# Four layers on one core: layer 3's sums in the scores' PSUM banks, another setup of layer 0, weights loaded within layer 0, and z's bias written into its bank by ScalarE

## The chip, the cores and the metric

The kernel runs on one core of one Trainium2 chip. The metric is the device time of one execution in microseconds, the median of several runs; lower is better. The profile of one execution has a span some 10 us under the median.

## The reference

64 graphs with 256 nodes and 256 features pass through four layers, each followed by a residual addition and a layer norm: `x = norm(x + layer(x, adj))`. All is float32.

- Layer 0 is a recurrence over the 256 nodes, for all graphs at once. Step i computes

```
x_par = sum_j adj[j, i] / d_j * h_j        # d_j: row sums of adj
r, z  = sigmoid(x_i @ W_ioux.T + b + x_par @ W_iouh.T + b)
hc    = tanh(x_i @ W_coux.T + b + (x_par * r) @ W_couh.T + b)
h_i   = z * x_par + (1 - z) * hc
```

  where `h_j` is the new state for j < i and the input for j >= i.
- Layer 1 is a graph convolution: `relu(D^-1/2 adj D^-1/2 (x W1.T + b1))`.
- Layer 2 is attention with one head and `adj` as a soft mask, followed by `Wo`, a bias and a relu.
- Layer 3 is attention with 8 heads of 32 features, with a score kept where `adj > 0`, then `Wo` and a bias.

## The kernel before

**Layer 0** (`_recurrence`). A setup loads and turns the weights, splits the bias into three bf16 parts (`bias3`) and writes the masks `window`. Then the part that doesn't depend on the recurrence, the contribution of the inputs to the first 128 nodes, is computed for all graphs in groups of GB = 8: `A` (L193) and `Xs` (L194) are loaded, `A` is masked on GpSimd, two matmuls a graph give `pb`, copies (half DVE, half ScalarE, L208) bring it to `ub`, and `x_out` stores it to DRAM `Us`. Then `degrees(0)` loads the first 32 rows of `adj` in four pieces through one buffer and computes `dinv`. `sums_in` loads from `Us` the accumulators `ACC` for 8 nodes each.

A step n, written out by hand (from here on each engine works in the order of the program): `xp` is transposed (`flip`), `h_part` adds its products with the weights to the PSUM tiles `rc` (gates r and c) and `z`, ScalarE takes the sigmoids, `rx` is transposed and gives c's second part, ScalarE takes tanh, DVE forms `zcc` (L815) and the next `xp` (L818). Between these PE computes the input products of the next step (`x_part`, L582). `rc` gets its bias by a ScalarE copy of `bias_rc` (L789), `z` by two small matmuls (`bias_part`, L573). Pushes of a new state into the accumulators of later nodes run on DVE (`ACC` L615) and GpSimd (`far` L647, `ACC` L651). States go through the tiles `hs` to a ring `Hw` of 64 nodes in SBUF (`into_ring`, in the steps p = n % 8 > 3) and from there to DRAM `Hd` (`flush`). Older states reach later nodes as "late" and "early" products, whose results pass through DRAM; `next_of(copies)` copies them out of PSUM on ScalarE, and `next_load` issues queued loads, two a step where p < 4.

**Layers 1 to 3** (`_layers`). All weights are loaded after the recurrence, W1 is turned, and the value bias of layer 3 is multiplied into its output bias (`bv`, L896 to L900). Then rounds: each advances five graphs, L, A, B, C and E, by one stage each, in the order of the string `ROUND`; `A.xT.1` is `Graph.xT(1)` of the graph in stage A. PSUM has four banks with the tag "mm", taken in turn by all products and transpositions (`bank`, `flipped`, `product` L948), and four, "sc0" to "sc3", for layer 3's scores (`s3`), one for each of four heads. `o3` takes two "mm" banks, and fills them with the sums of the exponentials (L1155) and the weighted values (L1164); `d3` divides on DVE (L1178 to L1180), `f3` applies `Wo`. `degrees_a` and `degrees_b` compute layer 1's `dis` (L1014), which `adT` needs on ScalarE.

A last part, `_layer_3`, runs only where a sum overflowed; it isn't entered here.

Of the kernel before, what the change touches and what calls it, by code (L numbers as in the profile page):

```python
# [19 lines left out]
P = 128  # L20
# [50 lines left out]
def _recurrence(tc, ident, Hd, x, adj, W_ioux, b_ioux, W_iouh, b_iouh, W_coux, b_coux, W_couh, b_couh):  # L71
# [31 lines left out]
    with ExitStack() as ctx:  # L103
# [6 lines left out]
        bias_rc = const.tile([P, 2, P], F32, name="bias_rc")  # L110
        tri = const.tile([P, P], F32, name="tri")
# [12 lines left out]
        with tc.tile_pool(name="r_setup", bufs=1) as tmp, tc.tile_pool(  # L124
            name="r_setup_ps", bufs=2, space=bass.MemoryType.PSUM
        ) as tps:
            for WT, wi, wc, s in ((WxT, W_ioux, W_coux, "x"), (WhT, W_iouh, W_couh, "h")):
                _load_wT(nc, tmp, tps, wi, ident, lambda c: WT[:, :, c % 2, c // 2 * 2, :], "i" + s)
                _load_wT(nc, tmp, tps, wc, ident, lambda c: WT[:, :, c, 1, :], "c" + s)
            bx, bh = (tmp.tile([1, 2, 3, P], F32, name=f"bias_{s}") for s in "xh")  # L130
            for t, bi, bc in ((bx, b_ioux, b_coux), (bh, b_iouh, b_couh)):
                for g in range(2):
                    nc.scalar.dma_start(
                        t[:, :, 2 * g, :],
                        bi[g * D:(g + 1) * D].rearrange("(c d) -> c d", c=2).unsqueeze(0),
                    )
                nc.scalar.dma_start(t[:, :, 1, :], bc.rearrange("(c d) -> c d", c=2).unsqueeze(0))
            nc.vector.tensor_add(bx, bx, bh)
            _split_bf16(nc, tmp, bias3, bx, "bias")

            span = tmp.tile([W, T // U, U], F32, name="span")
            nc.gpsimd.memset(span, 1.0)
            nc.gpsimd.affine_select(
                out=span, in_=span, pattern=[[U, T // U], [0, U]], compare_op=ALU.is_ge,
                fill=0.0, base=W - T // 2 - LAG - 1, channel_multiplier=-1,
            )
            for w in range(2):
                first = (w * T - W + T // 2) % W  # L150
                for lo, hi, at in ring(first, first + W):
                    for g in range(2):
                        nc.sync.dma_start(
                            window[w][g * W + at:g * W + at + hi - lo],
                            span[lo - first:hi - first].rearrange("p a u -> p (a u)"),
                        )
# [26 lines left out]


        with tc.tile_pool(name="r_first", bufs=2) as tmp, tc.tile_pool(
            name="r_first_ps", bufs=4, space=bass.MemoryType.PSUM
        ) as tps:
            for g in range(0, B, GB):
                A = tmp.tile([P, 2, GB, P], F32, tag="A", name=f"xA_{g}")
                Xs = tmp.tile([P, 2, GB, D], F32, tag="X", name=f"xX_{g}")  # L190
                for jc in range(2):
                    rows = slice(jc * P, (jc + 1) * P)
                    nc.sync.dma_start(A[:, jc], adj[g:g + GB, rows, 0:P].rearrange("b j i -> j b i"))  # L193
                    nc.scalar.dma_start(Xs[:, jc], x[g:g + GB, rows, :].rearrange("b j d -> j b d"))  # L194
                nc.gpsimd.tensor_mul(
                    A[:, 0], A[:, 0], tri.unsqueeze(1).to_broadcast([P, GB, P])
                )
                for n in range(0, GB, 4):
                    ub = tmp.tile([P, 4, D], F32, tag="ub", name=f"xu_{g}_{n}")
                    for e in range(0, 4, 2):  # L200
                        pb = tps.tile([P, 2, D], F32, tag="x", name=f"xp_{g}_{n}_{e}")
                        for q in range(2):
                            b = n + e + q
                            x_product(
                                pb, q, [A[:, jc, b, :] for jc in range(2)],
                                [Xs[:, jc, b, :] for jc in range(2)],
                            )
                        (nc.vector.tensor_copy if e else nc.scalar.copy)(ub[:, e:e + 2, :], pb)  # L208
                    x_out(0, g + n, ub)

        blk = ctx.enter_context(tc.tile_pool(name="r_blk", bufs=2))
        stream = ctx.enter_context(tc.tile_pool(name="r_stream", bufs=2))
        work = ctx.enter_context(tc.tile_pool(name="r_work", bufs=2))
        ps = ctx.enter_context(tc.tile_pool(name="r_ps", bufs=1, space=bass.MemoryType.PSUM))
# [24 lines left out]
        def load_later(out, in_, rank):  # L239

            begun = []

            def f(n):
                nc.sync.dma_start(out, in_)
                begun.append(n)

            loads.append((rank, f))
            loads.sort(key=lambda e: e[0])
            return begun
# [17 lines left out]
        def degrees(k):  # L267
# [16 lines left out]
            nc.vector.tensor_scalar(zero, deg, 0.0, None, ALU.is_equal)  # L284
            nc.vector.tensor_add(deg, deg, zero)
            nc.vector.reciprocal(deg, deg)
            nc.vector.tensor_scalar(zero, zero, -1.0, 1.0, ALU.mult, ALU.add)
            nc.vector.tensor_mul(deg, deg, zero)
            yield
            for h in range(2):  # L290
                at = k * T + h * HT
                for c in range(2):
                    nc.sync.dma_start(dinv[c * B:(c + 1) * B, at:at + HT], deg[h * B:(h + 1) * B])
# [69 lines left out]
        def early_load(e, got=[]):  # L363
# [5 lines left out]
            Hs = stream.tile([P, GB, D], F32, tag="Hs", name=f"Hs_{k}_{lo}_{t}", bufs=4)  # L369
# [258 lines left out]
        def state(n):  # L628
# [3 lines left out]
            hs = new("hs", n, 7)  # L632
# [4 lines left out]
        def into_ring():  # L637
            n, hs = ring_in.pop(0)
            for o in range(2):
                nc.sync.dma_start(Hw[n % W::W, :, o * P:(o + 1) * P], hs[o * B:(o + 1) * B])  # L640
# [19 lines left out]
        for _ in degrees(0):  # L660
            pass
        tables[0]["S"], double = load_S(0)
        double()
        tables[0]["Sd"] = chain_S(0)
        tables[0]["An"] = late_load(0)
        for a in range(3):
            sums_in(a)

        xq = {0: load_x(0)}
# [3 lines left out]
        xq[1] = load_x(1)  # L673
        rc = ps.tile([P, 2, P], F32, tag="rc", name="rc_0", bufs=2)
        z = ps.tile([P, P], F32, tag="z", name="z_ps_0")
        for G, gates in ((rc, slice(0, 2)), (z, 2)):
            bias_part(G, gates)
            if G is rc:
                nc.scalar.copy(bias_rc, rc)
# [29 lines left out]
        for now in range(N):  # L709
# [9 lines left out]
            if n:  # L719
# [13 lines left out]
                if p > 3:  # L733
# [67 lines left out]
            if not last:  # L801
# [6 lines left out]
                bias_part(z, 2)  # L808
# [29 lines left out]
            if i == 24:  # L838
                flush(n - 8 - T, n - 8)
            early_ahead(n)  # L840
# [14 lines left out]
        flush(N - T // 2, N)  # L855


def _layers(tc, ident, Hd, Yd, x, adj, w1, b1, l2, l3, out):
# [8 lines left out]
    nc = tc.nc  # L867
    B, N, D = x.shape
# [5 lines left out]
    with ExitStack() as ctx:  # L874
        const = ctx.enter_context(tc.tile_pool(name="l_const", bufs=1))
        W1T = const.tile([P, 2, D], F32, name="W1T")
        W2 = {n: _load_w(nc, const, l2["W" + n], f"W2{n}") for n in "qkvo"}
        W3 = {n: _load_w(nc, const, l3["W" + n], f"W3{n}") for n in "qkvo"}
        b1_r = _load_row(nc, const, b1, "b1_r")
        b2_r = _load_row(nc, const, l2["bo"], "b2o_r")  # L880
        b3_r = _load_row(nc, const, l3["bo"], "b3o_r")
        cols = const.tile([P, 6, 2], F32, name="b_cols")
        for s, b in enumerate((l2["bq"], l2["bk"], l3["bq"], l3["bk"], l3["bv"], l2["bv"])):
            _load_col(nc, cols[:, s, :], b)
# [5 lines left out]
        with tc.tile_pool(name="l_setup", bufs=1) as tmp, tc.tile_pool(  # L890
            name="l_setup_ps", bufs=2, space=bass.MemoryType.PSUM
        ) as tps:
            _load_wT(nc, tmp, tps, w1, ident, lambda c: W1T[:, :, c * P:(c + 1) * P], "w1")

            bv = tmp.tile([P, 2, P], F32, name="bv3")
            nc.vector.tensor_copy(bv, cols[:, 4, :].unsqueeze(2).to_broadcast([P, 2, P]))  # L896
            pb = tps.tile([P, D], F32, tag="wt", name="bv3_ps")
            for k in range(2):
                nc.tensor.matmul(pb, bv[:, k, :], W3["o"][:, k, :], start=(k == 0), stop=(k == 1))
            nc.vector.tensor_add(b3_r, b3_r, pb)  # L900
# [5 lines left out]
        ctx.enter_context(tc.manual_schedule())  # L906
# [23 lines left out]
        def bank(name, shape=(P, 2, D)):  # L930
            return ps.tile(list(shape), F32, tag="mm", name=name, bufs=4)

# [40 lines left out]
        class Graph:  # L973
# [7 lines left out]
            def load(self):  # L981
                b = self.b
                self.y = io.tile([P, 2, D], F32, tag="y", name=f"y_{b}", bufs=7)
                nc.sync.dma_start(self.y, Hd[:, b, :].rearrange("(c p) d -> p c d", p=P))
# [3 lines left out]
                nc.sync.dma_start(self.ad, adj[b].rearrange("(c p) m -> p c m", p=P))  # L988

# [158 lines left out]
            def o3(self):  # L1148


                self.o_ps = [bank(f"o3_{self.b}_{hc}") for hc in range(2)]
# [241 lines left out]
```

## Time and profile before

| | |
|---|---|
| time, median of 3 | 3578.55 us (3575.83 to 3585.26) |
| span of the profile | 3568.9 us |
| mean granted TensorE clock | 0.977 |
| busy: PE, DVE, ACT, POOL | 3223.1, 2465.2, 1900.3, 1874.5 us |
| chain that ended last | PE 61%, DVE 14%, DMA 6%, issue 6%, POOL 6%, ACT 5% |
| HBM read and written | 224.01 and 99.61 MB |

The busy times are over the whole span, whose stages have different limits. Four stages can be told apart in the slices of the page: the setup up to some 156 us, the steps of the recurrence up to 1563 us, a passage with little work up to some 1676 us, and the rounds up to the end. In the profile PE is a matmul, PEld a weight load, DVE VectorE, ACT ScalarE, POOL GpSimd, SPq the queue that issues DMAs from SyncE. An arrow names what a row reads or waits for.

### The profile page before, as it was taken

Reading aid. Unit: us, or ns where it says so; the run is one execution under the profiler, and the core shown is the slowest. Engines: PE = TensorE matmul, PEld = TensorE weight load, DVE = VectorE, ACT = ScalarE, POOL = GpSimd, SP = SyncE. Lnnn points to the kernel's source line nnn. Section 1 sums busy time; section 2 is a strip of 40 time slices with the busy share of each in tenths; the row PEclk is TensorE's granted clock in tenths of the full one; section 3 lists DMA queues with packets and bytes.
Section 4 is the critical chain, followed back from the end, with each engine's and each line's share of the span. In section 5 each row is a group of like instructions: output and inputs, shape, how many; then the busy total and the mean of one; then the engine's idle time right before and its main releaser. Section 6 shows DMA issues by size and latency. Waiting matters only on the chain.

```text
span 3568.9 us, 80419 instructions
## 1 busy us (share of the span) xinstructions
PE 3223.1 (90%) x29350; PEld 2318.4 (65%) x29350; DVE 2465.2 (69%) x7052; ACT 1900.3 (53%) x5026; POOL 1874.5 (53%) x2181
## 2 busy tenths in 40 slices
PE   5599999999989898858999999999999999999998
PEld 4455555555555555536777777777777777777775
DVE  2366767767667777735777777777777777777776
ACT  0155545545445454424666666666666666666664
POOL 2266677767667778723444444444444444444443
PEclk9799999999999999978999999999999999999999
DMA  8846566787876564140111111111111111111100
GB/s 281 224 132 144 162 174 152 162 190 201 201 191 166 154 152 120 58 116 18 45 45 45 45 45 45 45 45 45 45 45 45 45 45 45 45 43 45 45 27 22
DMA packets 389637, 348.43 MB, mean 98 GB/s; under 512 B 107244, under 2 KB 355192, under 8 KB 384120
## 3 DMA queue, kind: packets, MB, share of 16 engines
q1 hardware_dynamic: 367280, 323.84, 34.0%
q10 hardware_dynamic: 21960, 19.41, 1.6%
q8 instruction: 235, 3.85, 0.4%
q14 instruction: 162, 1.33, 0.1%
HBM read 224.01 MB, written 99.61 MB: 91 GB/s over the span
## 4 chain that ended last, share of the span: by engine, by line
PE 61%; DVE 14%; DMA 6%; issue 6%; POOL 6%; ACT 5%; SPq 2%; ACTq 0%; DVEq 0%; POOLq 0%
PE mm L948 13%; PE rc L590 4%; DVE p L1141 4%; PE s L1132 4%; PE rc L582 3%; PE mm_g L948 3%; PE mm_t L948 3%; PE mm_3f L948 3%; PE mm_3v L948 3%; PE mm_2s L948 3%; PE mm_2v L948 3%; PE late L506 3%; DVE ACC L615 3%; PE mm_2w L948 3%; POOL ACC L651 2%
## 5 line engine op out<-in xcount | busy, mean ns | idle before, releaser
L615 DVE SCALAR_TENSOR_TENSOR ACC<-keep,S,ACC 128x128 f32<-128x128 f32 x1712 | 504.8, 345 | 187.4 <-ACT hs L633 170.0
L1144 POOL TENSOR_TENSOR p3s<-p 128x256 f32<-128x256 f32 x512 | 387.8, 788 | 329.6 <-ACT p L1142 329.3
L925 ACT ACTIVATE y<-y,shift,rstd 128x256 f32<-128x256 f32 x512 | 273.4, 593 | 303.9 <-DVE shift L923 259.9
L1044 POOL TENSOR_TENSOR y<-y,g 128x512 f32<-128x512 f32 x64 | 81.1, 1267 | 601.1 <-issue 590.2
L651 POOL TENSOR_TENSOR ACC<-ACC,far 128x384 f32<-128x384 f32 (+1 forms) x313 | 371.3, 1186 | 24.6
L582 PE MATMUL rc<-WxT,xqT 128*64 128x256 f32 x2048 | 326.3, 397 | 6.1 <-ACT lb L232 1.7
L1141 DVE TENSOR_TENSOR p<-s,neg 128x512 f32<-128x512 f32 x512 | 317.7, 683 | 10.9 <-PE s L1132 8.8
L755 POOL TENSOR_TENSOR ready<-ACC,dinv 128x128 f32<-128x128 f32 x255 | 101.9, 400 | 391.3 <-DVE ACC L615 372.4
L647 POOL TENSOR_TENSOR far<-hs,S 128x384 f32<-128x384 f32 (+1 forms) x313 | 304.3, 972 | 4.7
L1142 ACT ACTIVATE p<-p 128x512 f32<-128x512 f32 x512 | 294.6, 624 | 2.6 <-DVE p L1141 1.6
L913 DVE BATCH_NORM_STATS2 st<-y 128x6 f32<-128x256 f32 x512 | 209.0, 408 | 95.0 <-POOL y L1044 90.2
L917 POOL TENSOR_TENSOR rstd<-rstd,mhalf 128x2 f32<-128x2 f32 x256 | 173.6, 695 | 125.7 <-DVE rstd L916 122.2
L1178 DVE RECIPROCAL rT<-o 128x256 f32<-128x256 f32 x128 | 223.8, 1748 | 0.3 <-PE o L1155 0.2
L599 ACT COPY xpT<-xpT_ps 128x128 f32<-128x128 f32 x256 | 68.3, 267 | 254.9 <-PE xpT_ps L597 254.9
L1164 PE MATMUL o<-p,v 128*32 128x256 f32 x2048 | 138.4, 382 | 70.8 <-ACT xT L1030 70.8
L590 PE MATMUL rc<-WhT,xpT 128*64 128x128 f32 x2048 | 170.7, 288 | 28.8 <-ACT xpT L599 28.6
L590 PEld LDWEIGHTS rc<-WhT,xpT 128*64 128x64 f32 x2048 | 108.1, 137 | 118.6 <-ACT xpT L599 84.1
L1187 DVE TENSOR_TENSOR y<-y,mm_3f 128x512 f32<-128x512 f32 x64 | 44.0, 688 | 187.9 <-PE mm_3f L948 187.9
L582 PE MATMUL z_ps<-WxT,xqT 128*64 128x128 f32 x2048 | 170.0, 287 | 0.0
L1107 ACT ACTIVATE qk<-mm,b_cols 128x256 f32<-128x256 f32 x256 | 107.5, 471 | 115.9 <-PE mm L948 115.9
L506 PE MATMUL late<-Hw,An 64*32 64x256 f32 x3840 | 154.9, 389 | 9.3 <-issue 4.4
L815 DVE TENSOR_TENSOR zcc<-zc,rc 128x128 f32<-128x128 f32 x256 | 72.7, 284 | 130.0 <-ACT rc L813 129.3
(168 smaller groups left out, 8004.6 us busy)
## 6 DMA issues: line engine op xcount, KB each, us to landing
xX<-in_x_dram ACTq DMA_DIRECT2D x16, 1024.0 KB
Us<-xu SPq DMA_DIRECT2D x64, 256.0 KB
rows<-in_adj_dram SPq DMA_DIRECT2D x64, 256.0 KB
ACC<-Us SPq DMA_DIRECT2D x32, 512.0 KB
xq<-in_x_dram SPq DMA_DIRECT2D x64, 256.0 KB
Hw<-hs SPq DMA_DIRECT2D x512, 32.0 KB
Es<-eu SPq DMA_DIRECT2D x64, 256.0 KB
early_sb<-Es SPq DMA_DIRECT2D x32, 512.0 KB
```

The source lines that it names most:

```text
L506: nc.tensor.matmul(pb[g][q * T:(q + 1) * T, e, :], An[rows, b].rearrange("p u s -> p (u s)"), Hw[rows, b, :], start=True, stop=True,)
L582: nc.tensor.matmul(G[o * B:(o + 1) * B], xqT[a, i // 2][:, i % 2, kc, h * B:(h + 1) * B], WxT[:, kc, o, gates], start=False, stop=False, s ...
L590: nc.tensor.matmul(G[o * B:(o + 1) * B], hT[:, kc * B:(kc + 1) * B], WhT[:, kc, o, g], start=False, stop=(kc == 1), skip_group_check=True,)
L615: nc.vector.scalar_tensor_tensor(acc[:, 0, :], keep[:, j % 2, :], s, acc[:, 0, :], ALU.mult, ALU.add)
L647: nc.gpsimd.tensor_mul(tmp[:, 0:count, :], hs.unsqueeze(1).to_broadcast(shape), s.unsqueeze(2).to_broadcast(shape),)
L651: nc.gpsimd.tensor_add(acc, acc, tmp[:, 0:count, :])
L925: nc.scalar.activation(y[:, c, :], y[:, c, :], AF.Identity, bias=shift[:, c:c + 1], scale=rstd[:, c:c + 1],)
L948: nc.tensor.matmul(pm[:, c, :], lhsT[:, k, c * P:(c + 1) * P], rhs[:, k, :], start=(k == 0), stop=(k == 1),)
L1141: nc.vector.tensor_add(p, s_ps[i], self.neg3)
L1142: nc.scalar.activation(p, p, AF.Exp, scale=ISQ)
L1144: nc.gpsimd.tensor_add(both, p[:, 0, :], p[:, 1, :])
L1178: nc.vector.reciprocal(rT, o_ps[:, 1, :])
```

## The change

It has four parts.

1. `o3` takes two of the scores' banks, sc0 and sc1, in place of two "mm" banks, so that these no longer lie between the transpositions and the products of the next graphs. In `ROUND`, `B.qk2.0` moves ahead of `C.norm_b.2` and `E.d3.1`, and `degrees_a` and `degrees_b` move from the end of a round into its first half.
2. The setup of layer 0: the first loads of `A` and `X` are issued ahead of everything, the weights are loaded after the first group and turned in the fourth, `degrees(0)` becomes one load of all 32 rows early on and one reduction in the third group, all copies out of PSUM are DVE's, and the tiles `X` come from a pool `wide` that also serves the early products' `Hs`.
3. The weights of layers 1 to 3 are loaded by `next_load` in the last 40 steps, into three tiles of `wide`. The last 8 states are stored straight to `Hd` and not through the ring, in every one of these steps. In `load`, `y` comes after `xin` and `ad`.
4. `z` gets its bias by a ScalarE copy of `bias_z`, as `rc` does. The ring of `hs` tiles has 6 and not 7.

The core of the diff:

```diff
+        first_in = [first_load(g) for g in (0, GB)]
+        rows_0 = fst.tile([P, T // 2, N], F32, name="rows_0", bufs=1)
...
-                        (nc.vector.tensor_copy if e else nc.scalar.copy)(ub[:, e:e + 2, :], pb)
+                        nc.vector.tensor_copy(ub[:, e:e + 2, :], pb)
                     x_out(0, g + n, ub)
+                if g + 2 * GB < B:
+                    first_in.append(first_load(g + 2 * GB))
+                if g == 0:
+                    load_weights()
+                if g == 3 * GB:
+                    turn_weights()
+                if g == 2 * GB:
+                    deg = fst.tile([P, T // 2], F32, name="deg_0", bufs=1)
+                    nc.vector.tensor_reduce(deg, rows_0, AX.X, ALU.add)
...
-            hs = new("hs", n, 7)
+            hs = new("hs", n, 6)
...
-                nc.sync.dma_start(Hw[n % W::W, :, o * P:(o + 1) * P], hs[o * B:(o + 1) * B])
+                to = Hw[n % W::W] if n < N - U else Hd[n]
+                nc.sync.dma_start(to[..., o * P:(o + 1) * P], hs[o * B:(o + 1) * B])
...
-                if p > 3:
+                if p > 3 or n >= N - U:
                     for _ in range(min(2, len(ring_in))):
                         into_ring()
...
                 z = ps.tile([P, P], F32, tag="z", name=f"z_ps_{n + 1}")
-                bias_part(z, 2)
+                if n:
+                    nc.scalar.copy(z, bias_z)
+                else:
+                    bias_part(z, 2)
...
+            if n == N - U + 3:
+                flush(N - T // 2, N - U)
+            if n == N - 5 * U:
+                then(lambda to, of: load_later(to, of, 3))
...
-                self.o_ps = [bank(f"o3_{self.b}_{hc}") for hc in range(2)]
+                self.o_ps = [
+                    ps.tile([P, 2, N], F32, tag=f"sc{hc}", name=f"o3_{self.b}_{hc}", bufs=1)
+                    for hc in range(2)
+                ]
...
-            A.xT.1 B.xT.2 E.o3 E.d3.0 C.norm_b.2 E.d3.1 B.qk2.0
-            A.t B.qk2.1 B.v2 L.residual_0 B.masks
-            E.f3 C.xT.3 A.g C.bias_3 L.norm_a.0
+            A.xT.1 B.xT.2 E.o3 E.d3.0 B.qk2.0 C.norm_b.2 E.d3.1
+            A.t B.qk2.1 B.v2 L.residual_0 B.masks L.degrees_a
+            E.f3 L.degrees_b C.xT.3 A.g C.bias_3 L.norm_a.0
             C.qk3.0 C.qk3.1 E.norm_a.3 A.norm_a.1 L.norm_b.0 B.s2 B.exp2
-            C.s3.0 C.v3 B.w2 L.degrees_a
-            B.pT2 E.norm_b.3 E.store A.norm_b.1 C.s3.1 B.f2 L.degrees_b
+            C.s3.0 C.v3 B.w2
+            B.pT2 E.norm_b.3 E.store A.norm_b.1 C.s3.1 B.f2
             L.adT B.norm_a.2
```

## The prediction

> **What bounds the kernel now.** I first cut the span into stages with the busy time by window (columns: stretch, its length, then busy us and instruction counts of PE, PEld, DVE, ACT, POOL, then granted clock, DMA share, GB/s).
>
> ```profile
> 0.00:156.00 156.00, 83.65 (x319) 64.45 (x321) 29.83 (x53) 12.47 (x21) 32.98 (x27) 0.83 0.86 267
> 157.00:1563.00 1406.00, 1279.69 (x16471) 757.28 (x16467) 974.94 (x3344) 699.81 (x2444) 959.94 (x1064) 0.99 0.62 154
> 1563.00:1676.00 113.00, 64.40 (x304) 49.56 (x308) 38.13 (x108) 35.46 (x77) 25.57 (x32) 0.71 0.30 79
> 1676.00:3480.00 1804.00, 1722.87 (x11789) 1394.06 (x11780) 1368.39 (x3429) 1111.86 (x2400) 827.86 (x1022) 1.00 0.14 44
> ```
>
> Setup is DMA (0.86 busy), the 256 recurrence steps are PE and a latency chain, the 113 us between the recurrence and the steady rounds are mostly idle, and the rounds of layers 1 to 3 are TensorE (1722.87 of 1804.00, 95.5%). So each part of the change has a stage of its own.
>
> Setup and the passage between layers, in the chain of waits (start, us, what):
>
> ```profile
> 99.47 0.70 DVE xu L208
> ...
> 123.18 4.20 DMA rows<-in_adj_dram
> 127.50 1.29 DVE deg L279 x2
> 128.81 0.49 SPq L276
> 129.34 4.23 DMA rows<-in_adj_dram
> ...
> 1563.67 2.60 DMA Hw<-hs
> 1566.64 10.37 DMA Hd<-Hw
> ...
> 1580.82 5.26 DMA W3o<-in_L_gnn_Wo_dram
> 1586.10 2.90 DMA b_cols<-in_L_gnn_bv_dram
> 1589.42 2.06 PE bv_ps L899 x4
> 1591.92 3.10 DMA xin<-in_x_dram
> 1595.18 1.27 POOL y L992
> ```
>
> Four degree loads run one after the other with nothing beside them (122 to 148 us). After the last state, flush, weights, the bias product and the first graph's loads follow each other for 32 us.
>
> The round, in the timeline of PE (idle before and its releaser in brackets):
>
> ```profile
> 2752.95 0.64 PE L1155 MATMUL o<-p3s,ones 128*32 128x256 f32 x8 [0.20 <-POOL p3s L1144]
> 2753.38 1.07 PE L1164 MATMUL o<-p,v 128*32 128x256 f32 x16
> 2755.60 1.07 PE L1164 MATMUL o<-p,v 128*32 128x256 f32 x16 [1.15 <-ACT xT L1030]
> ```
>
> and what PE waited for between 1676 and 3480 us:
>
> ```profile
> PE o L1164 <- ACT xT L1030: 69.4, 60, 1.2
> PE o L1155 <- POOL p3s L1144: 10.5, 53, 0.2
> ```
>
> PE idles once per round, in front of `heads(1)` of `o3`, 1.15 us in 60 rounds, and 0.20 ahead of `sums(0)`. A round takes 30.01 us (2725.59 to 2755.60), of which PE is busy 28.66.
>
> **What the Trainium skill says.** "DMA: Bandwidth & Descriptors", section Rules for kernel authors: spreading DMAs over issuing queues gives no bandwidth, all share the same 16 engines. The trace agrees: with two queues the windows show 352 GB/s at a DMA share of 1.09 between 22 and 113 us. So bytes set the setup's length. "PSUM — Partial Sum Buffer", section Terms: eight banks of 2 KiB a partition. Here four "mm" and four "sc" banks fill all eight, so the o3 sums can get other banks only by sharing. The same page, section The four PSUM rules: ScalarE writes neither set nor clear the written bits, so a later accumulating matmul adds to what ScalarE wrote where they are set. The kernel before does this for `rc` already (L789). "TensorE: Matmul & The Clock Gate", section What's actually happening: the clock halves after about 3.4 us of idling. The trace agrees: after the passage `mm_t` needs 3.80 us for 8 matmuls, in the rounds 1.73.
>
> **Part 1, layer 3's sums in the scores' banks.** The five banks taken in a row (`tr_ad`, two `tr_x`, two `o`) don't fit in four, so the second `o` waits until `adT` and `xT` on ACT have read. ACT itself waited 0.61 us for DVE `dis` L1014, which stands behind the last scores and `f2`. After the change `o` takes sc0 and sc1. Their readers, the first two `p` additions of the scores, end at 2750.8 (2749.53 plus two of 0.6), before PE needs the banks at 2752.75. The order also takes `dis` out of the way: `degrees_a` goes behind `t`, where DVE idles 2.98 us for `mm_3f`, and `degrees_b` behind `f3`.
> What comes next, in the round's own times: PE ends the transpositions at 2752.75, then 0.55 + 0.90 + 0.90 for `sums(0)` and both `heads` gives 2755.1. `sums(1)` needs the last `p3s`, which POOL ends at 2755.48 (2752.20 + 3.28), so PE ends about 2755.65. `qk2.0` needs the second `xT`; ACT ends its exponentials at 2753.62 and, no longer waiting, adT and both xT 1.8 later, 2755.42. So PE starts `qk2.0` near 2755.65 and not at 2757.03: 1.3 to 1.35 less, the whole idle time. The d3 reads hold sc0 and sc1 to about 2760.8, `s3.0` needs them at 2743 + 28.7 = 2771.7. The 60 rounds of the wait row by 1.3 make 78 us. Ends: 40 (a wait of 0.65 left) and 81 (60 x 1.35).
>
> **Part 2, setup.** Removed from the path: 21 us of weights, bias split and windows ahead of the first adjacency load (issued at 21.05), and the degree stage. Added to the stage's bytes: rows 2.10 MB, weights 1.57, S twice about 0.6, 4.3 MB; at 352 GB/s 12.1 us. The first part lasts from 21.05 to the landing of the last `Us` at 122.3, 101.3 us. Starting at 0.8 it ends at 0.8 + 101.3 + 12.1 = 114.2. Then xq (0.6 + 3.75 us in the chain), `ACC`, xp, a transposition, h_part and the table load (1.28): I add 2 x 0.6 for the xq issues ahead, 5 for `ACC`, and 5 for the rest, and get the first sigmoid at 125.5, against 157.83. Gain 32; between 22 (copies now all on DVE, 32 x 0.69, and the single in-order SP queue cost 10) and 40 (the bytes fill gaps of the old stream).
>
> **Part 3, passage.** The last state goes straight to Hd: the 10.37 us flush, the weights and `bv` leave the path, and xin and ad are ahead of y in the queue. Last hs copy 1563.1, issue 0.5, landing 2.6, y's issue 0.5 and landing 3.1: the first `y` addition at 1569.9 and not 1595.18, 25 us. The filling rounds lose their `dis` wait ahead of `adT` (0.64 and more in each): 2 more, 27 in all, between 22 and 30. The 18 weight loads are spread over the last five groups of steps, whose SP queue has no early pieces left.
>
> **Part 4, z's bias.** Out: 2 matmuls on PE, 0.17 us a step (926.44 to 926.61). In: one ScalarE copy of 128x128, 0.27 us by the hs copy (L633), in front of tanh. In the timeline of 255 steps I took the time from the end of `xp` (L818) to its transposition: 0.05 to 0.06 in 96 steps (xp is last), 0.10 to 0.12 in 124 (PE is last, by 0.05), 0.6 in 31 (p = 4, where `flip_x` follows; PE is last by 0.54), longer in 4. So 124 x 0.05 + 31 x 0.17 = 11.5 us could come. The copy waits for DVE `keep` L795; behind it on ACT stand tanh and, through zcc and xp, the next step. ACT idles 0.27 to 0.29 us for `rc` ahead of tanh even after a 0.59 us copy, and the copy's start-to-start is 0.17, so it fits; where two copies stand there (p = 3) zcc waits for DVE `ACC` anyhow. Blocks with a DMA stall at p = 5 to 7 take part of it back. I take 7; ends +11 and -20 (0.08 a step left on the path). The hs ring of 6 and not 7 leaves at least 9 us between a store's issue and the reuse by the step times, and a store lands in 2.6: nothing.
>
> **Sum.** 78 + 32 + 27 + 7 = 144; 3578.55 - 144 = 3434.5 us.
>
> **Rivals.**
> A new wait takes the bank's place: p3s or the second xT ends later than I count, and half a wait, 0.65, stays. For it: ACT is without a gap from 2744.51 on, and POOL's last p3s is at PE's heels (2755.48 against 2755.45). Against: both end before 2755.65. Then 144 - 39 = 105, 3473.5 us.
> Setup is hidden anyway: the stream stays bound by stores that wait in one SP queue (chain: DVE xu behind `Us` again and again), and gains only 10. For it: `ub` keeps two buffers. Against: DMA moves 352 GB/s all the while. Then 144 - 22 = 122, 3456.5.
> Slower: the copy of z comes fully onto the step (254 x 0.27 = 69 lost and the 7 not won) and the scores wait for d3, so that 60 rounds grow by 2.6, one d3's reciprocal, product and maximum (156 lost, 78 not won). For it: DVE holds sc1 until d3.1. Against: 11 us of slack there. Then 32 + 27 - 69 - 156 = -166, 3744.5 us.
>
> **How the numbers follow.** My forecast 0.70, the new wait 0.15, the setup 0.10, slower 0.05. The predicted time is the forecast's. The range takes in the new wait (3473.5) and, below, all upper ends at once short of a few us (81 + 40 + 30 + 11 = 162, 3416): 3412 to 3478. Faster by over 0.3% (10.7 us) is true of the first three, 0.95 less 0.01 for mixtures: 0.94; same 0.01; slower 0.05.
>
> **What would show it.** Right: PE's row "o L1164 <- ACT xT L1030" gone or under 10 us, a round of 28.7 us, DMA `rows` off the chain ahead of the first step, first sigmoid near 125 us, the first `y` addition about 7 us after the last hs copy, PE without L573 but for the first steps, and steps of p = 4 shorter by 0.17. Wrong: a new releaser of `o` or `qk2.0` with 0.5 us or more a round, `ACC` or `xq` landing after 122 us, tanh waiting for the z copy, or hs copies waiting for stores.

## The result and the profile after

| | before | after |
|---|---|---|
| time, median of four | 3580.93 us (3575.83 to 3585.26) | 3462.05 us (3457.94 to 3474.60) |
| span of the profile | 3568.9 us | 3457.8 us |
| first sigmoid of the steps | 157.83 | 142.68 |
| first sigmoid to the last `hs` copy | 1405.00 | 1404.51 |
| last `hs` copy to the first `y` addition | 32.35 | 7.03 |
| first `y` addition to the fifth `mm_t` | 113.29 | 109.36 |
| fifth `mm_t` to the end | 1860.43 | 1794.22 |
| median round | 30.01 | 28.85 |

The ratio is 0.9674 (95% interval 0.9645 to 0.9704), 118.9 us less between the medians. The two profiled executions differ by 111.1 us, since that of before took 3570.75 us, less than any of the four in the table. The stages are from these two: 15.2 + 0.5 + 25.3 + 3.9 + 66.2 = 111.1 us. So the rounds bring the most, the passage what was forecast, the setup half, the steps nothing.

The busy time by window of the changed kernel, in the steps and in the rounds from the fifth `mm_t` on (stretch, length, then busy us and counts of PE, PEld, DVE, ACT, POOL, then clock, DMA share, GB/s; the share is the packets' times added up, over the stretch and 16 engines, and can pass 1):

```profile
143.00:1547.00 1404.00, 1215.92 (x15957) 767.34 (x15957) 973.65 (x3344) 744.12 (x2695) 960.79 (x1066) 0.98 0.63 157
1664.00:3457.00 1793.00, 1775.11 (x12037) 1427.11 (x12035) 1427.40 (x3487) 1126.58 (x2445) 839.79 (x1040) 1.00 0.13 44
```

and of the kernel before, from its fifth `mm_t` on:

```profile
1708.00:3568.00 1860.00, 1763.75 (x12041) 1421.64 (x12040) 1397.58 (x3488) 1133.52 (x2445) 840.98 (x1040) 1.00 0.13 43
```

In the steps PE has lost 64 us of work (1279.69 to 1215.92), and the stage is as long as it was: the sum of PE's work doesn't set it. In the rounds, with the same work, PE is now busy 99% of the time, where it was 94.8%.

The same place of a round in PE's timeline of the changed kernel, and POOL's beside it:

```profile
2726.29 0.64 PE L1212 MATMUL o<-p3s,ones 128*32 128x256 f32 x8
2726.75 1.91 PE L1221 MATMUL o<-p,v 128*32 128x256 f32 x32
2728.48 1.08 PE L1212 MATMUL o<-p3s,ones 128*32 128x256 f32 x8
2729.49 0.70 PE L1002 MATMUL mm<-xT,weights 128*128 128x256 f32 x2
```

```profile
2725.63 3.26 POOL L1198 TENSOR_TENSOR p3s<-p 128x256 f32<-128x256 f32 x4 [2.93 <-ACT p L1196]
```

The 1.15 us gap ahead of `heads(1)` is gone. The second `sums` takes 1.08 us where the first takes 0.64 for as many matmuls: it is stretched by the last `p3s`, which POOL ends at 2728.89 (2725.63 + 3.26). What PE's weight loads waited for in the rounds shows it too (total us, times, longest us):

```profile
PEld o L1212 <- POOL p3s L1198: 23.2, 64, 0.9
```

The passage, in the chain of waits:

```profile
1547.19 0.28 ACT hs L651
1547.48 0.45 SPq L659
1547.97 0.60 SPq L659
...
1548.67 2.89 DMA xin<-in_x_dram
1551.60 2.59 issue
1554.22 1.26 POOL y L1046
```

Flush, weight loads and bias product no longer stand between `hs` and `y`. The end of the setup, in the same view:

```profile
95.34 9.46 DMA xA<-in_adj_dram
...
118.24 7.19 PE xp L213 x32
...
126.57 2.52 DMA Us<-xu
...
131.85 6.77 DMA ACC<-Us
...
138.71 0.63 DVE xp L736
```

The `rows` loads are gone from it, but the last `Us` lands at 129.1, and the forecast had 114.2.

### The profile page after: what moved, and what is told of

It reads as the page before. It is cut to its first block, busy times and chain, and to the rows that moved or that the text cites. A ratio compares the mean times of both kernels' runs of the same rounds, so it can differ in the third digit from the quotient of the medians.

```text
span 3457.8 us, 79283 instructions
## 1 busy us (share of the span) xinstructions
PE 3165.8 (92%) x28842; PEld 2331.9 (67%) x28842; DVE 2502.2 (72%) x7061; ACT 1929.9 (56%) x5265; POOL 1873.7 (54%) x2181
## 4 chain that ended last, share of the span: by engine, by line
PE 69%; DVE 9%; DMA 7%; POOL 5%; issue 4%; ACT 4%; SPq 2%; ACTq 0%; DVEq 0%; POOLq 0%
PE mm L1002 13%; PE rc L608 5%; PE s L1186 4%; PE mm_2f L1002 4%; PE mm_3v L1002 3%; PE mm_t L1002 3%; PE mm_3f L1002 3%; PE late L524 3%; PE mm_2v L1002 3%; PE mm_g L1002 3%; PE mm_2s L1002 3%; DVE ACC L633 3%; PE mm_2w L1002 3%; PE o L1221 3%; PE o L1212 3%
## 5 line engine op out<-in xcount | busy, mean ns | idle before, releaser
L1002 PE MATMUL mm<-xT,weights 128*128 128x256 f32 x2048 | 481.8, 383 | 2.9 <-ACT xT L1084 2.9
L1002 PEld LDWEIGHTS mm<-xT,weights 128*128 128x128 f32 x2048 | 384.7, 190 | 79.6 <-issue 25.5
L1109 ACT ACTIVATE qk<-mm,weights 128x256 f32<-128x256 f32 x256 | 107.5, 471 | 268.3 <-PE mm L1002 268.3
L1063 POOL TENSOR_TENSOR dis<-dis,mhalf 128x2 f32<-128x2 f32 x64 | 44.8, 700 | 277.1 <-DVE dis L1062 260.7
L1161 ACT ACTIVATE qk<-mm,weights 128x256 f32<-128x256 f32 x256 | 107.5, 471 | 115.9 <-PE mm L1002 115.9
L213 PE MATMUL xp<-xX,xA 128*128 128x256 f32 x384 | 110.7, 426 | 66.9 <-POOL xA L686 39.8
```

The lines of the kernel that those rows point to most:

```text
L1002: nc.tensor.matmul(pm[:, c, :], lhsT[:, k, c * P:(c + 1) * P], rhs[:, k, :], start=(k == 0), stop=(k == 1),)
```

## Experiments

Those on the rounds change the changed kernel in one place each.

**Banks.** `o3` back in two "mm" banks, the new order kept:

```diff
-                self.o_ps = [ps.tile([P, 2, N], F32, tag=f"sc{hc}", ...) for hc in range(2)]
+                self.o_ps = [bank(f"o3_{self.b}_{hc}") for hc in range(2)]
```

> The changed kernel with o3's sums back in two of the four mm banks; the new order of the round stays. Theory A (the bank wait and the wait of adT for dis are two links of one chain): without dis in the way adT and xT on ScalarE come 0.6 us earlier, so of the old idle 1.15 us about half stays; a round of 29.3 to 29.5 us, 30 us more than the changed kernel, about 3492 us. Rival (the bank alone made the whole wait): a round of 30.0 us, about 3532 us. Rival (the order alone made it): 28.85 us, 3462 us.

Measured: 3474.38 us, a round of 29.08: midway between theory A and the rival of the order alone. PE's wait rows of it:

```profile
PE o L1218 <- ACT xT L1084: 12.6, 54, 0.5
PE o L1209 <- DVE f L1150: 10.4, 53, 0.2
```

**Order.** The new banks, with `ROUND` of before:

```diff
-            A.xT.1 B.xT.2 E.o3 E.d3.0 B.qk2.0 C.norm_b.2 E.d3.1
+            A.xT.1 B.xT.2 E.o3 E.d3.0 C.norm_b.2 E.d3.1 B.qk2.0
```

(and `degrees_a`, `degrees_b` back at their old places.)

> The changed kernel with the old order of the round; o3's sums stay in the scores' banks. Theory A: adT waits for dis again, the second xT ends about 0.6 us later, near 0.05 us before the place where qk2.0 starts now; a round of 28.85 to 29.0 us, 0 to 9 us more than the changed kernel. Rival (the order is needed for the gain): a round of 29.4 us or more, 33 us more, 3495 us.

Measured: 3474.09 us, a round of 29.07, just above what theory A allowed. PE's weight loads waited

```profile
PEld o L1212 <- POOL p3s L1198: 28.9, 53, 0.6
PEld mm L1002 <- ACT xT L1084: 21.8, 53, 0.4
```

In the changed kernel the first row is 18.0 us over the same number of rounds, and the second isn't there.

Of the 1.16 us that a round gains, the order alone brings 0.93 and the banks alone 0.93. They are two ways out of one chain: with the order alone the wait for `xT` is 0.2 us a round (12.6 over 54), since ACT reads the banks sooner; with the banks alone `heads(1)` doesn't wait for `xT`, but the weight loads of `qk2.0` do, by 0.4 us a round, since ACT still stands 0.61 us ahead of `adT` and comes to `xT` later. The last 0.2 needs both.

**The last sums behind `B.qk2.0`.** `sums(1)` becomes a stage `E.o3_last` after the products:

```diff
-            A.xT.1 B.xT.2 E.o3 E.d3.0 B.qk2.0 C.norm_b.2 E.d3.1
+            A.xT.1 B.xT.2 E.o3 E.d3.0 B.qk2.0 E.o3_last C.norm_b.2 E.d3.1
```

> The changed kernel with sums(1) of o3 issued behind B.qk2.0 and not ahead of it. Theory B (what is left idle in a round is the wait of sums(1) for GpSimd's last p3s): qk2.0 starts as soon as the second xT has been copied, and the round goes from 28.85 to 28.6 to 28.7 us; 9 to 15 us less, 3447 to 3453 us. Rival (the second xT on ScalarE ends the wait as well): 28.85 us still, no change.

Measured: 3461.04 us, a round of 28.91, nothing gained: the rival. The wait for `p3s` goes over to the next:

```profile
PEld mm L1002 <- ACT xT L1084: 32.1, 53, 0.6
```

So two releasers end at nearly the same time there; POOL's alone isn't worth removing.

**Setup.** Seven arrangements of its loads and buffers, layer 0's steps and all else as in the changed kernel. For a measure of the scatter: the five runs on other parts, whose setup is that of the changed kernel, have their first sigmoid between 140.3 and 143.7. First in program order (the changed kernel leaves the order of this stage to a scheduler), with rows, `S`, windows and the degree reduction behind groups 2 to 5 (the edits of this and the next two are moves of those calls):

> The changed kernel with its setup in the order of the program, and the rows of adj, S, the window masks and the degree reduction put behind the second to fifth group. Theory C (the setup lost 17 us against my count because DVE's reduction stood ahead of the first copies and waited for rows, and the SyncE queue stood in the window transfers until 32.5 us, so that the third group of A was issued at 42): first sigmoid at 125 to 130 us and not at 142.7, 12 to 17 us less, 3445 to 3450 us. Rival (DMA bytes and stores bind the setup anyway): first sigmoid at 139 us or later, at most 4 us less.

Measured: 3469.61 us, the first sigmoid at 148.93, so the rival, and later than before the move. The weight and bias issues now stood between the stores of one group and the next, and behind `rows` and `S` a single `Us` issue took 11.11 us.

Then all that the groups don't need at groups 4 to 6:

```diff
-                if g == 0:
+                if g == 4 * GB:
                     load_weights()
```

> The setup of layer 0 in program order, and everything that the eight groups don't need themselves put behind them: the weights and biases are issued with group 4, the rows for the degrees and S with group 5, the mask windows and the degree reduction with group 6, so that SyncE's queue holds only group loads and U stores before that. Theory A (what stands in SyncE's queue between the stores of one group and the loads of the next sets the setup: 20.26 us for the eight window issues in the changed kernel, 24 us of waits in the first hand-made order): the first sigmoid at 128 to 136 instead of 142.68, so 7 to 15 us less than the changed kernel, 3447 to 3455. Rival B (two U buffers and one group load of 1 MB at a time bind anyway, or the moved loads only come out at the end, where ACC, the inverse degrees and the windows are waited for): the first sigmoid at 140 to 150, time 3460 to 3470.

Measured: 3455.55 us, the first sigmoid at 139.50: sooner by 3.2, half of the least that theory A gave, and just outside of the scatter. The products ended by 102, but the last stores stood behind a bias part (one issue of 11.02 us), windows and inverse degrees in SyncE's queue until 122.

The same, with `A` loaded through ScalarE's queue:

```diff
-                nc.sync.dma_start(A[:, jc], adj[g:g + GB, rows, 0:P].rearrange("b j i -> j b i"))
+                nc.scalar.dma_start(A[:, jc], adj[g:g + GB, rows, 0:P].rearrange("b j i -> j b i"))
```

> As the run before, with the A loads of the groups issued by ScalarE's queue beside the x loads, so that no store and no other load stands ahead of them. Theory A1 (a load of A behind the wait of a store for its U is a further part of the loss): 3 to 8 us less than the run before, the first sigmoid at 124 to 130. Rival B1 (the buffers of A, free only after the group's products, are what the load waits for in any queue): within 2 us of the run before.

Measured: 3463.95 us, the first sigmoid at 137.62. With that 1.9 us sooner, rival B1 holds for the setup. The median time is 8.4 us above that of the run before, with overlapping ranges and 6.8 us more in the steps, whose code is the same.

Small transfers on ScalarE's queue, so that SyncE has only `A` and `Us`:

```diff
-                nc.sync.dma_start(nat[name], w.rearrange("(c p) d -> p c d", p=P))
+                nc.scalar.dma_start(nat[name], w.rearrange("(c p) d -> p c d", p=P))
```

(likewise windows, biases, `bias3`, rows, `S`, `dinv`.)

> SyncE's queue left to the A loads and the stores of U in the setup: the mask windows are issued by ScalarE behind its first x loads, the weights and biases behind the x loads of group 6, the rows, S and its copy behind those of group 7, the three bias parts and the inverse degrees by ScalarE too; otherwise as in the run with all extras last. There, of the time from the last xu (101) to the first sigmoid (139.5), 8.6 us were a bias part and some 7 us twelve small issues in SyncE's queue, ahead of the last stores of U. Theory A (the queue's order is what is left): the last stores are issued at 103 to 106 instead of 124, the first sigmoid at 120 to 128, the time 3436 to 3446. Rival B (the rows, the inverse degrees or the raw block set the end at the same place whichever queue issues them): the first sigmoid at 134 to 140, the time 3450 to 3458.

Measured: 3459.46 us, the first sigmoid at 138.70: rival B, with the time 1.5 us above its range. The last eight stores still spread over 19.78 us from 102.76: in the chain the `rows` load (16.88 us to its landing) and the degree reduction now stand on VectorE ahead of the last `xu` copies.

**Windows alone later,** from ahead of the groups to group 2:

```diff
+                if g == 2 * GB:
+                    load_windows()
```

> The changed kernel with one edit: the eight window issues stand behind group 2 in the program instead of ahead of the first stores of U. Theory A (the eight issues, 20.26 us at 12 to 32 us, hold the first stores and with them all later groups): the first sigmoid 8 to 15 us sooner, 128 to 135. Theory B (the issues wait there only because the loads ahead of them are still landing, and whatever stands next in the queue would wait as long): the first sigmoid within 3 us of 142.7.

Measured: 3455.25 us (3453.07 to 3461.57), the first sigmoid at 140.22: theory B. SyncE's timeline of the changed kernel has the first line, that of this run the others:

```profile
12.27 20.26 SPq L194 DMA_DIRECT2D window<-span  x8
```

```profile
7.39 4.77 SPq L146 DMA_DIRECT2D rows<-in_adj_dram  x2
12.21 0.66 SPq L548 DMA_DIRECT2D S<-in_adj_dram  x1
12.91 16.83 SPq L159 DMA_DIRECT2D nat_ix<-in_L_gnn_W_ioux_dram  x1
```

A different transfer now waits at the same place, a single issue 16.83 us.

**More buffers,** on top of the windows later: four of `xu`, or three of `A` (the edit of the latter is `bufs=3` and a third group loaded ahead):

```diff
-                    ub = fst.tile([P, 4, D], F32, tag="ub", name=f"xu_{g}_{n}")
+                    ub = fst.tile([P, 4, D], F32, tag="ub", name=f"xu_{g}_{n}", bufs=4)
```

> The run with the windows later, with one more edit: the tile xu that the copies of the products go to has four buffers instead of two, so that a copy of the products need not wait for the store of the products two before it. In the run with the windows later VectorE waited 17.9 us for stores of U (29.0 us in the changed kernel). Theory A (two U buffers hold the groups back): these waits fall under 5 us and the first sigmoid comes 5 to 12 us sooner, at 128 to 135, the time 3443 to 3450. Rival B (the loads set the pace: after 12 us the engines move 330 to 370 GB/s in most stretches, and from the landing of the last A to xp pass 21 us of work in a row): the waits go over to another row and the first sigmoid stays within 3 us of 140.

> The run with the windows later, with the A tile of a group in three buffers instead of two and three groups' A loads issued ahead; the x tiles keep their four buffers, which is two groups. GpSimd waited 63.7 us for A loads there, each issued only after the products of two groups before. Theory A (the distance of two groups from a load to its use sets the pace): the waits for A fall to under 40 us, the first sigmoid at 128 to 135. Rival B (x loads, 2 MB a group against 1 MB of A, wait for buffers as before, and the stream's rate is the limit): the first sigmoid within 3 us of 140.

Measured: 3462.60 us and 145.35, and 3455.45 us and 140.14. What VectorE and GpSimd waited for up to 138 us, with four `xu` buffers and then with three of `A`:

```profile
POOL xA L689 <- DMA xA<-in_adj_dram: 87.4, 6, 27.9
DVE xu L702 <- PE xp L216: 65.6, 25, 18.3
```

```profile
POOL xA L689 <- DMA xA<-in_adj_dram: 58.7, 6, 23.9
DVE xu L702 <- DMA Us<-xu: 30.2, 9, 10.2
```

With four buffers no wait for a store is left among the long rows, and the loads of `A` are waited for 24 us more than with two (63.7). With three of `A` the wait for its loads falls by 5 us alone, and that for stores grows from 17.9 to 30.2. So theory A fails both times. Rival B holds for `A`; for `xu` the waits moved as it says, but the first sigmoid came 2.4 us later than it allows.

**z's bias.** The bf16 products again:

```diff
-                if n:
-                    nc.scalar.copy(z, bias_z)
-                else:
-                    bias_part(z, 2)
+                bias_part(z, 2)
```

> z's bias written by its bf16 products again, hs still in a ring of 6, all else as in the changed kernel. Theory A (the copy is worth 11 us in the medians of positions p = 4 and p = 0, and lone stalls of steps by transfers, which the copy has no part in, ate it): the medians go back to about 5.51 and 5.31, the stalls stay as in the changed kernel, so that the time is 3470 to 3476. Rival B (the shorter steps only run into the transfers that the stalls wait for: what is gained in the medians is lost there whatever the copy does): the medians go back, the stalls fall by as much, and the time stays at 3460 to 3465. Rival C (the copy lengthens other steps): 3455 or less.

The same with the old ring (`new("hs", n, 7)`) and no `bias_z`:

> z's part undone whole: the bf16 products, no bias_z, and hs in a ring of 7 as before. If the smaller ring makes part of the stalls, the sum of the steps' excess over their medians is 4 to 10 us less than in the run before, and the time by as much less; if not, it is within 2 us of the run before.

Measured: 3467.21 us (3458.59 to 3475.93) and 3465.74 us (3461.96 to 3466.95). The sum of the steps from step 1 on, from one transposition of `xp` to the next in PE's timeline, is 1397.3 us before, 1396.9 after, 1413.6 with the products and the ring of 6, 1404.6 with the products and the ring of 7. The medians at p = 4 and p = 0 went from 5.51 and 5.31 (before) to 5.16 and 5.20 (after), and with the products back to 5.51 and 5.31. What ScalarE's `hs` copies waited for in the steps, for the changed kernel, for products with the ring of 6, and with 7:

```profile
ACT hs L651 <- DMA Hw<-hs: 7.4, 4, 3.9
```

```profile
ACT hs L651 <- DMA Hw<-hs: 4.0, 4, 1.6
```

```profile
ACT hs L650 <- DMA Hw<-hs: 0.7, 1, 0.7
```

Before has no such row. The ten other runs with the copy and the ring of 6 show 7.4 to 16.4 us of it, and sums of the steps between 1394.7 and 1408.3, though their steps are the same code. In the profiles the copy is worth 16.7 us and the ring costs 9.0, but each is one pair of executions with that scatter. The steps' excess over the medians of their positions points the same way for the ring: 68.8 and 73.2 us in the two executions with a ring of 7 (before, and the last run), 74.4 to 87.8 in the twelve with 6. The times differ by 5.2 and 1.5 us, with overlapping ranges, between theories A and B of the first run and under what the second had forecast, so how much of either reaches the total stays open.

## Why the prediction was right, and where it was off

3434.5 was forecast, 3462.05 came: faster, as forecast, and inside the range, but with 111 us gained in the profiles and not 144. The range was wide enough because it took in the rival with half a wait left (3473.5). The time lies between that and the second rival (3456.5, the setup gains only 10), nearest to the latter, but the reason given there doesn't hold: four `xu` buffers took the waits for stores away, and the first sigmoid came no sooner (145.35). By the steps of the sum, in the two profiles:

| | forecast | measured |
|---|---|---|
| rounds | 78 | 66.2 |
| setup | 32 | 15.2 |
| passage and filling | 27 | 29.2 |
| z's bias | 7 | 0.5 |

- **Passage.** Right in each link: 7.03 us from `hs` to `y`, and 3.9 in the filling.
- **Rounds.** The mechanism was right; the term "1.3 to 1.35 less, the whole idle time" was too large, 1.16 measured. It let PE end `sums(1)` 0.17 us after POOL's last `p3s` and start `qk2.0` at once. In the trace `qk2.0` starts 0.60 after it (2728.89 to 2729.49). The first rival, a new wait in the bank's place, is partly true.
- **Setup.** The failed term is "4.3 MB; at 352 GB/s 12.1 us", on top of an unchanged stream: the last `Us` landed 15 us after the 114.2 forecast, and the rest of the stage took 13.6 and not 11.3. The like stretches, from the first loads to the last store of the groups, before and after:

```profile
21.00:122.00 101.00, 70.12 (x260) 55.92 (x260) 11.07 (x16) 11.03 (x18) 18.77 (x8) 0.90 1.03 333
```

```profile
1.00:129.00 128.00, 73.13 (x284) 58.32 (x284) 37.56 (x60) 1.82 (x3) 26.66 (x15) 0.85 0.99 296
19.00:28.00 9.00, 3.23 (x15) 2.49 (x14) 0.00 (x0) 0.00 (x0) 0.00 (x0) 0.81 1.01 217
28.00:32.00 4.00, 0.59 (x2) 0.50 (x3) 1.66 (x1) 0.00 (x0) 0.00 (x0) 0.50 0.41 72
```

  The 4.3 MB were right (333 x 101 against 296 x 128), their price wasn't: they took 22 us of all engines' time (0.99 x 128 against 1.03 x 101), not 12.1. By the times of the packets in the trace, of these ten us too few 3.5 belong to `rows`: its 2.1 MB come in 128 packets of 16 KB of 1.19 us each, and while they come in the engines are full at 217 GB/s (the second line after), not 352. Packets of 1 KB took 50 ns on average and not 47, 3.9 us more. Those under 512 B took 1.9 us more than at 352 GB/s. The Trainium skill, "DMA: Bandwidth & Descriptors", section Why small descriptors are slow (HBM only), states a fixed overhead for each packet; the trace agrees in direction, 16 ns for 128 bytes. The other 5 us of the loss are engines less full. About half of that is the hole behind `rows`: until 32.5 us SyncE's queue issued no store, and the engines ran half empty (the third line).
  What the experiments show is that neither the place of the extra loads in the queue, nor the issuing queue, nor one more kind of buffer sets the setup by itself: seven other arrangements gave a first sigmoid between 137.6 and 148.9, and where a wait was taken away, another one grew. All seven kept the load of `rows` as it is. In the run with all extras last it came in at 218 GB/s as well, between 100 and 108 us, with the issue behind it held. What another form of this load would bring was not tried and stays open.
- **z's bias.** The forecast of the regular part came near in its sum, not in its parts. By the medians it is some 14 us, 0.35 in each of 32 steps at p = 4 and 0.10 at p = 0, against 11.5. The time from the end of `xp` to its transposition did fall by 0.05 us in the 124 steps, but they stand at four positions, and at three of these the step got no shorter. At p = 4 it fell by 0.32 and not 0.17, so that the sum came near in part by luck. "The hs ring of 6 ... nothing" failed. The "at least 9 us between a store's issue and the reuse" is the old ring's: in the traces it is 9.3 us at the least before, and 2.2 in the changed kernel. There `hs` copies wait for stores of `Hw`, by up to 3.9 us. That wait is in step 158, which is 3.3 us longer than before; but it is 2.7 longer with products and a ring of 7 as well, so not all of it is the ring's. Single long steps, which add up to 9.0 us more than before, took back most of what the copy brought. Which part the ring has in it isn't settled.

Three runs (extras last, windows later, three `A` buffers) have medians near 3455.5, 6.5 us under the changed kernel; their ranges overlap its own, so none is shown to beat it.

## What to carry to other kernels

Where two edits shorten one wait, price the pair, not the sum: each alone gave 80% of what both give. A load that is added to a stream doesn't come at the stream's rate: take its own rate from a trace, and look at which issue of the queue stands behind it. And before shortening a ring by one, look at the whole time from a tile's write to the store's landing, with the queue ahead of the store in it.

## What the runs showed of the hardware

Single DMA issues were held up for long. In each of the seven other arrangements of the setup one issue took 8.63 to 16.88 us, where no other up to 145 us took over 5.3. Each time it is the one behind the two issues of `rows` and that of `S`, on SyncE's queue or, in the run with small transfers there, on ScalarE's, and it has no data in common with them. It ended 0.3 to 0.8 us after the last packet of `rows`. In the changed kernel the eight window issues of a few KB stand behind `rows` and take 20.26 us in all, where they take 5.09 later on (5.95 when moved to group 2); there the row of waits names landings of `xX`, `xA` and `rows`. That it is `rows`, and not `S`, which holds the issue isn't shown: no run parts them.

The rate of full DMA engines went with the load: 371 GB/s at a share of 1.10 for the rows of 512 B and 1 KB between 4 and 18 us, 217 at 1.01 for the 16 KB of `rows` between 19 and 28.
